# Float16 weights straight from dequantization, and new homes for the cross-attention and FFN tiles, in a one-core decoder layer

## The chip, the cores and the metric

The kernel runs on one core of a Trainium2 chip. The core has five engines that run side by side and meet through semaphores: TensorE (PE, matrix products into PSUM), VectorE (DVE), ScalarE (ACT), GpSimd (POOL) and SyncE (SP, which issues the DMAs). The metric is the device time of one launch in microseconds (us), the median of several runs. Before the change it is 676.97 us (three runs, 676.77 to 679.08).

## What is computed

One decoder layer over x of 8 batches x 128 rows x 512 columns, with a layer norm ahead of each of three parts:

```
x = x + attn(layernorm(x))             # 32 query heads, 8 key/value heads, head size 128, causal softmax
x = x + xattn(ctx, ctx, layernorm(x))  # sim = softmax(ctx @ q.T / 8), softmax over the query index; out = sim @ ctx
x = x + ffn(layernorm(x))              # gate, up: 512 -> 1376; down: 1376 -> 512
ffn:  W[k,n] = q[k,n]*s[g,n] - (z[g,n]+1)*s[g,n],  g = k // 128      # 4-bit q and z, one scale per group of 128
      inter = gate * sigmoid(gate) * up;  out = float16(inter @ Wd)
```

## The kernel before

**Number form.** Every float32 operand of a product is split into two float16 halves, "hi" and "lo" (`split`, `convert`), and a product is three matmuls, hi\*hi, hi\*lo and lo\*hi (`mm3`). The integer weights of the FFN (q - 1 - z) are exact in one float16, so an FFN round has two matmuls: weight x hi, weight x lo.

**Steps.** The attention runs in 64 steps, one for each pair of a key/value group g and a batch b. A step issues on PE the scores (`att_s`), the projections for a later unit of four steps (`proj_parts`), the output projection of the step before (`att_o`) and the product with V (`att_v`). Beside the steps, work is attached to step numbers: weights of the next groups are fetched and converted, the 35 chunks of quantized weights are unpacked in steps 8 to 42 (`dequant`: a shift-and-mask and one scalar_tensor_tensor on VectorE, result in the int8 tiles `n8`), and from step 43 (`XC`) on the context of the cross-attention is loaded (`c_load`), measured (`sumsq`), scaled on GpSimd and split (`c_prep`).

**The tail.** The last group's steps 52 to 55 and 60 to 63 finish one batch each. One step after a batch is done comes `xA` (transposes of the context and of the normed row block by DMA), another step later `xB` (scores and softmax of the cross-attention), then `xC` (its product with the context), with `h3_load`, the layer norm that feeds the FFN.

**The FFN.** From step 60 (`FFN0`) on, FFN rounds are put between attention pieces from a list of events sorted by slot, four slots to a step. `gate_up` makes 22 chains for each half of four batches (11 column tiles x gate, up), each of four rounds, one per quantization group. Between two rounds the PSUM accumulator is multiplied by a ratio of scales, on ScalarE and VectorE in turn, so a chain's next round waits for that. Chain c starts at slot c, its rounds one slot apart. A finished gate chain ends in Silu on ScalarE; an up chain in a product on VectorE, a float16 copy (hi) on VectorE and a subtraction (lo) mostly on GpSimd, into the tile `it`. `down` then makes four chains of eleven rounds.

**Weight copies.** Before its use in the FFN, `nf_load` turns each gate tile from int8 to float16 on ScalarE and each up tile on VectorE (11 + 11), from steps 47 to 55, tiles 3 to 10 into buffers of the attention's query weights (`wqp`); `down_w` does so with 11 down tiles on ScalarE, from steps 52 to 62.

**What sets the order.** The program lists instructions in the order of the code; a planner then orders each engine's queue by readiness and that order. An order written out by hand holds in the tail: PE from step 53 up to step 60, GpSimd from step 53 to the last attention step. Each engine works its queue in order, and SP issues all DMAs of the kernel.

**Pools.** Tiles live in pools that are released and replaced: `deqp` (dequantization) gives way to `xa` (all cross-attention tiles) at step 43, `rawp` (raw weights) to `fw` (float16 FFN weights) and `fp` at step 52 (`FFN_MEM`), and `xa` gives way to `late` (output tiles) near the end. A tile in a replaced pool waits for the last readers of the tiles that it lies upon.

Of the kernel before, what the change touches and what calls it, by code (L numbers as in the profile page):

```python
# [8 lines left out]
F32 = mybir.dt.float32  # L9
F32R = mybir.dt.float32r  # L10
F16 = mybir.dt.float16
BF16 = mybir.dt.bfloat16
I32 = mybir.dt.int32
I8 = mybir.dt.int8
AF = mybir.ActivationFunctionType
ALU = mybir.AluOpType
PSUM = bass.MemoryType.PSUM

P = 128
HQ = 64  # L20
B = 8
H = 512
# [26 lines left out]
XPSCALE = 2.0**15  # L49
ROOT = 2.0**-104  # L50

NF0 = 3


@with_exitstack
def tile_decoder(
# [473 lines left out]
    def run(gen):  # L530
        for _ in gen:
            pass
# [72 lines left out]
    def att_o(g, b):  # L605
# [11 lines left out]


    sF = {}
    n8 = {  # L620
        "g": nqp.tile([P, KT, INTER], I8, name="n8g"),
        "u": nqp.tile([P, KT, INTER], I8, name="n8u"),
        "d": nqp.tile([P, NFT, H], I8, name="n8d"),
    }
    quant = {
        "g": (gq, gz, gs, KT, INTER),
# [111 lines left out]
    def dequant(m, g, c0, c1, after):  # L738
        qsrc = quant[m][0]
        n = c1 - c0  # L740
        rows = min(16, qsrc.shape[0] - g * 16)
        p = rows * 8
        qr = deqp.tile([P, H], I32, name="qr", tag="qr", bufs=2)
        nc.sync.dma_start(
            qr[:p, :n],
            qsrc[g * 16 : g * 16 + rows, c0:c1]
            .rearrange("r n -> r () n")
            .to_broadcast([rows, 8, n]),
        )
        zi = deqp.tile([P, H], I32, name="zi", tag="zi", bufs=2)  # L750
        row = zrow[m] + g
        nc.sync.dma_start(
            zi[:p, :n],
            zt["d"][row : row + 1, c0:c1].to_broadcast([p, n]),
        )
        qi = deqp.tile([P, H], I32, name="qi", tag="qi", bufs=1)
        ins = nc.vector.tensor_scalar(
            qi[:p, :n], qr[:p, :n], sh[:p], 15, ALU.logical_shift_right, ALU.bitwise_and
        )
        issue_after(ins, after)  # L760
        nc.vector.scalar_tensor_tensor(
            n8[m][:p, g, c0:c1], qi[:p, :n], -1.0, zi[:p, :n], ALU.add, ALU.subtract
        )

    chunks = []
# [143 lines left out]
            issue_after(ins, pace["dma"])  # L909

    def c_load(b):
        raw_t["c", b] = c = xa.tile([P, H], F32, name="c", tag="c", bufs=3)
        nc.sync.dma_start(c, cx[b])

    def c_prep(b):
        scales("c", b)
        ctx_scale(b)
        c = raw_t.pop(("c", b))
        ins = nc.gpsimd.tensor_tensor(
            c, c, scx[:, b : b + 1].to_broadcast([P, H]), ALU.mult  # L920
        )
        issue_after(ins, pace["mul"])
        cp = xa.tile([P, 2, H], F16, name="cp", tag="cp", bufs=B)
        split(cp[:, 0, :], cp[:, 1, :], c, nc.gpsimd)
        fl["c", b] = cp

    def norm_T(b, dst):
# [75 lines left out]
    for b in range(B):  # L1003
        at_x(XC + b, lambda b=b: c_load(b))
        at_x(XC + b + 1, lambda b=b: sumsq("c", b, 0, 0))
        at_x(XC + b + 3, lambda b=b: c_prep(b))
        done = steps.index((NG - 1, b))
        tail_x.setdefault((done + 1, 0), []).append(lambda b=b: xA(b))
        tail_x.setdefault((done + 2, 1), []).append(lambda b=b: xB(b))
        tail_x.setdefault((done + 3, 0), []).append(lambda b=b: (xC(b), h3_load(b)))  # L1010

    nf = {}

    def nf_load(m, t):
        w = min(P, INTER - t * P)
        if t < NF0:
            nf[m, t] = fw.tile([P, KT, P], F16, name="nf", tag="nf", bufs=2 * NF0)
        else:
            nf[m, t] = wqp.tile(
                [P, KT, P], F16, name="nf", tag={"g": "wqh", "u": "wql"}[m]  # L1020
            )
        src = n8[m][:, :, t * P : t * P + w]
        if m == "g":
            nc.scalar.copy(nf[m, t][:, :, :w], src)
        else:
            nc.vector.tensor_copy(nf[m, t][:, :, :w], src)

    h3 = {}

# [100 lines left out]
    def gate_up(half, t, m):  # L1130
        w = min(P, INTER - t * P)

        def parts(g):
            return nf[m, t][:, g, :w], h3[half][:, 0, g, :], h3[half][:, 1, g, :]

        def finish(ps):
            sc = sF[m][:w, t, :]
            if m == "g":
                sg = fp.tile([P, TH], F32, name="sg", tag="sg")
                nc.scalar.activation(sg[:w], ps, AF.Silu, scale=sc)  # L1140
                sg_t[half, t] = sg
                return
            sg = sg_t.pop((half, t))
            pr = fp.tile([P, TH], F32, name="pr", tag="pr")
            nc.vector.scalar_tensor_tensor(pr[:w], ps, sc, sg[:w], ALU.mult, ALU.mult)
            if t < NFT - 1:
                it = qp.tile([P, 2, TH], F16, name="it", tag="q" + "hl"[t % 2])
            else:
                it = fw.tile([P, 2, TH], F16, name="it", tag="it", bufs=1)
            eng = nc.vector if half and t >= NFT - 2 else nc.gpsimd  # L1150
            nc.vector.tensor_copy(it[:w, 0, :], pr[:w])  # L1151
            eng.tensor_tensor(it[:w, 1, :], pr[:w], it[:w, 0, :], ALU.subtract)  # L1152
            it_t[half, t] = it

        return Chain(KT, w, lambda: rT[m][:, t, :], parts, finish)

    nd_t = {}

    def down_w(g):
        w = min(P, INTER - g * P)  # L1160
        nd_t[g] = fw.tile([P, H], F16, name="nfd", tag="nfd", bufs=NFT)
        nc.scalar.copy(nd_t[g][:w], n8["d"][:w, g, :])

    def down(half, ct):
        cs = slice(ct * P, (ct + 1) * P)

        def parts(g):
            w = min(P, INTER - g * P)
            it = it_t[half, g]
            return nd_t[g][:w, cs], it[:w, 0, :], it[:w, 1, :]  # L1170

        def finish(ps):
            o = late[0].tile([P, TH], F32, name="oT", tag="oT", bufs=4)
            sc = sF["d"][:, ct, :]
            if ct % 2:
                nc.scalar.activation(o, ps, AF.Copy, scale=sc)
            else:
                nc.vector.tensor_scalar(o, ps, sc, None, ALU.mult)
            pt = bank("a", [P, HB, P], "ps_f")
            for bb in range(HB):  # L1180
                nc.tensor.transpose(pt[:, bb, :], o[:, bb * P : (bb + 1) * P], ident)
            o16 = late[0].tile([P, HB, P], F16, name="o16", tag="o16", bufs=2)
# [12 lines left out]

    late = []

    def free_xa():
        xa.release()
        late.append(pool("late", side="right", reuse_waits="tile"))  # L1200


# [5 lines left out]
    for half, (gs_, ds_) in enumerate([(0, D0), (G1, D1)]):  # L1208
        for c in range(NC):
            ch = gate_up(half, c // 2, "gu"[c % 2])  # L1210
            st = gs_ + (c if half else c + min(c, EARLY))
            for r in range(KT):
                events.append((st + r, 1, c, lambda ch=ch, r=r: ch.emit(r)))
        for ct in range(KT):
            ch = down(half, ct)
            for r in range(NFT):
                st = ct * (0.5 if half else 1)
                events.append((ds_ + st + r, 1, NC + ct, lambda ch=ch, r=r: ch.emit(r)))
    for i, k in [i for i in tail_x if i[0] >= len(steps)]:
        slot = PER_STEP * (i - FFN0) + 1 + 2 * k  # L1220
        events.append((slot, 0, 1, lambda fs=tail_x.pop((i, k)): [f() for f in fs]))
    events.append((PER_STEP * (len(steps) + 5 - FFN0), 0, 1, free_xa))
    events.sort(key=lambda e: e[:3])

    def traced_after(n, engine, earlier):
# [16 lines left out]
    def tail_step(i):  # L1242
# [14 lines left out]
        for f in tail_x.pop((i, 0), ()):  # L1257
            f()
        run(parts)
        slots(3)  # L1260
        att_v(g, b)
        slots(4)
# [15 lines left out]
    for i in range(len(steps)):  # L1278
        known = len(nc.cur_bb.bb.instructions)
        if i == XC:  # L1280
            deqp.release()
            xa = pool("xa", 2, side="right", reuse_waits="tile")
        if i == FFN_MEM:
            rawp.release()
            fw = pool("fw", reuse_waits="tile")
            fp = pool("fp", 2, reuse_waits="tile")
        if i == FFN0:
            xt.update(s="a", o="a")
        pace["dma"] = pt_dma[steps[i + 1]] if i >= TAIL and steps[i + 1 :] and steps[i + 1] in pt_dma else None
# [17 lines left out]
            inter_scale()  # L1307
        for f in x_steps.pop(i, ()):
            f()
        for t in range(NFT):  # L1310
            if i == (FFN_MEM + 1 + t if t < NF0 else XATT - 4 + t):
                nf_load("g", t)
                nf_load("u", t)
        for g in range(NFT):
            if i == FFN_MEM + g:
                down_w(g)
        if i < 5 * HB:
            traced_after(known, last_h.ins.engine, last_h)
        if i == TAIL - 1:
# [8 lines left out]
    for e in events:  # L1328
        e[3]()

    for pl in (late[0], wvp, wkp, wqp, hp, fp, fw, qp, kp, vp, work, wop, psum, dram, nqp):
        pl.release()
    for pl in (small, xres, const):
        pl.release()
# [50 lines left out]
```

## Time and profile before

| | value |
|---|---|
| median of three runs | 676.97 us |
| the profiled execution, its own time | 678.71 us |
| its span, first to last instruction | 676.7 us |
| PE busy | 639.2 us, 94% |
| DVE busy | 480.2 us, 71% |
| ACT busy | 453.2 us, 67% |
| POOL busy | 400.6 us, 59% |
| DMA queue q1 | 42.7% of 16 engines' time |
| mean granted PE clock | 0.989 |

The profile of one execution gives, for each engine, when each instruction started and how long it took; a line number (L...) is that of the kernel's source, and where a helper such as `split` issues the instruction, it is the helper's line. PE instructions overlap, so a PE that is "busy" can still be short of its full rate; how close it is shows in how far apart the starts of neighbouring matmuls lie. Two neighbouring 512-column matmuls start 0.216 us apart where nothing holds them up.

### The profile page before, as it was taken

Reading aid. Unit: us, or ns where it says so; the run is one execution under the profiler, and the core shown is the slowest. Engines: PE = TensorE matmul, PEld = TensorE weight load, DVE = VectorE, ACT = ScalarE, POOL = GpSimd, SP = SyncE. Lnnn points to the kernel's source line nnn. Section 1 sums busy time; section 2 is a strip of 40 time slices with the busy share of each in tenths; the row PEclk is TensorE's granted clock in tenths of the full one; section 3 lists DMA queues with packets and bytes.
Section 4 is the critical chain, followed back from the end, with each engine's and each line's share of the span. In section 5 each row is a group of like instructions: output and inputs, shape, how many; then the busy total and the mean of one; then the engine's idle time right before and its main releaser. Section 6 shows DMA issues by size and latency. Waiting matters only on the chain.

```text
span 676.7 us, 12449 instructions
## 1 busy us (share of the span) xinstructions
PE 639.2 (94%) x3978; PEld 341.6 (50%) x3978; DVE 480.2 (71%) x1504; ACT 453.2 (67%) x1261; POOL 400.6 (59%) x583
## 2 busy tenths in 40 slices
PE   8798999999999999999999999989989988999995
PEld 4365555455555555555555564544545443444442
DVE  6756587765757777676768464676777767988996
ACT  4587486655657574666667666796666667978674
POOL 5658287844747795555588497876775426521310
PEclk9988999999999999999999999999999999999998
DMA  9266344665453756455554525224433232202002
GB/s 309 49 154 176 97 62 117 163 126 148 112 155 87 188 128 157 104 159 127 160 142 109 134 37 136 54 57 87 84 74 56 55 59 48 47 16 62 1 1 62
DMA packets 117757, 69.34 MB, mean 102 GB/s; under 512 B 84174, under 2 KB 100577, under 8 KB 117692
## 3 DMA queue, kind: packets, MB, share of 16 engines
q1 hardware_dynamic: 117692, 68.55, 42.7%
q8 instruction: 31, 0.51, 0.3%
q14 instruction: 34, 0.28, 0.1%
HBM read 42.12 MB, written 2.20 MB: 65 GB/s over the span
## 4 chain that ended last, share of the span: by engine, by line
PE 54%; POOL 14%; DVE 9%; ACT 9%; issue 7%; DMA 6%; SPq 0%; POOLq 0%; DVEq 0%; ACTq 0%
PE ps_o L165 5%; PE ps_c L1114 5%; PE ps_o L163 5%; PE ps_o L164 5%; PE ps_c L1115 5%; PE ps_q L163 5%; PE ps_q L164 5%; PE ps_q L165 4%; DMA pt<-pb 3%; POOL pb L120 3%; POOL s L574 2%; DVE ps_c L1125 2%; POOL wol L120 2%; POOL rawo L357 1%; POOL wql L120 1%
## 5 line engine op out<-in xcount | busy, mean ns | idle before, releaser
L517 ACT ACTIVATE s<-s,negm 128x64 f32<-128x64 f32 (+1 forms) x256 | 93.2, 366 | 35.3 <-DVE negm L560 35.1
L165 PE MATMUL ps_o<-woh,al 128*128 128x512 f16 x256 | 97.3, 380 | 3.4 <-DVE al L120 3.2
L163 PE MATMUL ps_o<-woh,ah 128*128 128x512 f16 x256 | 97.3, 380 | 2.1 <-ACT ah L117 1.9
L163 PE MATMUL ps_q<-hT,wqh 128*128 128x512 f16 x256 | 97.4, 380 | 1.9 <-DVE ql L120 1.0
L165 PE MATMUL ps_q<-hT,wql 128*128 128x512 f16 x256 | 97.3, 380 | 0.0
L164 PE MATMUL ps_o<-wol,ah 128*128 128x512 f16 x256 | 97.3, 380 | 0.0
L164 PE MATMUL ps_q<-hT,wqh 128*128 128x512 f16 x256 | 97.3, 380 | 0.0
L614 DVE SCALAR_TENSOR_TENSOR xr<-ps_o,unsc,xr 128x512 f32<-128x512 f32 x64 | 47.8, 747 | 45.9 <-PE ps_o L165 42.4
L120 POOL TENSOR_TENSOR pb<-s,pb 128x256 f16<-128x256 f32 (+1 forms) x128 | 73.0, 585 | 10.3 <-ACT pb L117 8.6
L560 DVE CUSTOM_DVE_ANT_0 s<-ps_sc,mask,soft 128x64 f32<-128x64 f32 (+1 forms) x256 | 67.2, 310 | 7.3 <-PE ps_sc L165 6.6
L1114 PE MATMUL ps_c<-h,nf 128*128 128x512 f16 (+1 forms) x176 | 66.6, 379 | 3.9 <-ACT sg L1140 1.6
L1115 PE MATMUL ps_c<-h,nf 128*128 128x512 f16 (+1 forms) x176 | 66.6, 379 | 0.0
L574 POOL TENSOR_TENSOR s<-s,rec 128x128 f32<-128x128 f32 (+1 forms) x128 | 62.7, 510 | 4.5
L117 ACT CAST pb<-s 128x128 f16<-128x128 f32 (+1 forms) x128 | 43.2, 350 | 32.3 <-POOL s L574 31.1
L527 POOL TENSOR_SCALAR rec<-rec 128x4 f32<-128x4 f32 x64 | 14.7, 230 | 82.7 <-DVE rec L525 80.5
L120 DVE TENSOR_TENSOR ql<-ps_q,qh 128x512 f16<-128x512 f32 x64 | 43.9, 686 | 25.5 <-ACT qh L117 25.1
L1152 POOL TENSOR_TENSOR it<-pr,it 128x512 f16<-128x512 f32 (+1 forms) x20 | 23.1, 1154 | 63.9 <-DVE it L1151 53.3
L357 POOL TENSOR_TENSOR rawo<-rawo,sco 128x512 f32<-128x512 f32 x30 | 31.1, 1038 | 29.3 <-DVE sco L313 29.3
L120 DVE TENSOR_TENSOR al<-ps_at,ah 128x512 f16<-128x512 f32 x64 | 43.8, 684 | 6.5 <-ACT ah L117 6.3
L517 ACT ACTIVATION_READ_ACCUMULATOR s<-s,negm 128x1 f32 x256 | 48.1, 188 | 0.0
L117 ACT CAST ah<-ps_at 128x512 f16<-128x512 f32 x64 | 37.2, 581 | 14.8 <-PE ps_n L291 7.1
L1123 ACT ACTIVATE ps_c<-ps_c,rTu 128x512 f32<-128x512 f32 (+1 forms) x57 | 36.7, 661 | 12.9 <-PE ps_c L1115 12.3
(219 smaller groups left out, 1733.8 us busy)
## 6 DMA issues: line engine op xcount, KB each, us to landing
rawq<-in_L_attn_w_q_dram SPq DMA_DIRECT2D x8, 1024.0 KB, 6.5
rawo<-in_L_attn_w_o_dram SPq DMA_DIRECT2D x8, 1024.0 KB, 5.4
zi<-zd SPq DMA_DIRECT2D x26, 256.0 KB, 3.7
vd<-v SPq DMA_DIRECT2D x64, 64.0 KB, 2.4
qr<-_L_ffn_down_qweight_dram SPq DMA_DIRECT2D x10, 256.0 KB, 3.3
xr<-in_x_dram SPq DMA_DIRECT2D x8, 256.0 KB, 5.2
rawk<-in_L_attn_w_k_dram SPq DMA_DIRECT2D x8, 256.0 KB, 3.3
rawv<-in_L_attn_w_v_dram SPq DMA_DIRECT2D x4, 512.0 KB, 7.7
```

Source lines behind the costliest of these rows:

```text
L117: a = nc.scalar.copy(hi, src)
L120: b = (lo_eng or nc.vector).tensor_tensor(lo, src, hi, ALU.subtract)
L163: nc.tensor.matmul(ps, lh, rh, start=start and i == 0, stop=False)
L164: nc.tensor.matmul(ps, lh, rl, start=False, stop=False)
L165: nc.tensor.matmul(ps, ll, rh, start=False, stop=stop and i == n - 1)
L357: a = nc.gpsimd.tensor_tensor(raw, raw, wide.to_broadcast(list(raw.shape)), ALU.mult)
L517: exp = nc.scalar.activation(v, v, AF.Exp, bias=negm[:, j : j + 1], scale=-1.0, accum_out=sums[:, j : j + 1],)
L560: nc.vector.tensor_tensor_reduce(view, flat(ps, cols[j]), masks[j // 2], soft_t[g][:, j % 2 : j % 2 + 1], BIG, ALU.add, ALU.min, negm,)
L574: mul = nc.gpsimd.tensor_tensor(v, v, rec[:, 2 * k : 2 * k + 2].unsqueeze(2).to_broadcast([P, 2, (k + 1) * HQ]), ALU.mult,)
L614: return nc.vector.scalar_tensor_tensor(xr[b], ps, unsc_t[g], xr[b], ALU.mult, ALU.add)
L1114: nc.tensor.matmul(ps, lh, rh, start=r == 0, stop=False, skip_group_check=r > 0)
L1115: nc.tensor.matmul(ps, lh, rl, start=False, stop=True, skip_group_check=r > 0)
```

## The change

Six edits, in the order of the code:

- The dequantized weights are kept as float16 for the whole kernel (`nf`, three tiles) instead of int8 (`n8`), and the 33 later copies (`nf_load`, `down_w`) are gone.
- The context lives in a pool of its own, `xc`, opened at step 43 where `xa` was; the other cross-attention tiles (`xa`) move to the pool space opened at step 52, in place of `fw`.
- `c_prep` calls `convert(..., True)`: hi is a scaled copy on ScalarE, lo a scalar_tensor_tensor on VectorE, both straight from the raw context. GpSimd's multiplication and subtraction go.
- `xC` and `h3_load` of the first three batches are issued after the step's projections instead of before.
- The rounds of a gate or up chain lie 1.25 slots apart instead of 1, but for the first seven chains of the first half.
- `it`: of the 22 tiles of the two halves, number 8 to 17 take the query buffers of `qp`, the others the freed query-weight buffers of `wqp`. In the second half the first nine hi copies move from VectorE to GpSimd.

```diff
-    n8 = {
-        "g": nqp.tile([P, KT, INTER], I8, name="n8g"),
+    nf = {
+        "g": nqp.tile([P, KT, INTER], F16, name="nfg"),
...
         nc.vector.scalar_tensor_tensor(
-            n8[m][:p, g, c0:c1], qi[:p, :n], -1.0, zi[:p, :n], ALU.add, ALU.subtract
+            nf[m][:p, g, c0:c1], qi[:p, :n], -1.0, zi[:p, :n], ALU.add, ALU.subtract
         )
...
-        raw_t["c", b] = c = xa.tile([P, H], F32, name="c", tag="c", bufs=3)
+        raw_t["c", b] = c = xc.tile([P, H], F32, name="c", tag="c", bufs=3)
...
-        ins = nc.gpsimd.tensor_tensor(
-            c, c, scx[:, b : b + 1].to_broadcast([P, H]), ALU.mult
-        )
-        issue_after(ins, pace["mul"])
-        cp = xa.tile([P, 2, H], F16, name="cp", tag="cp", bufs=B)
-        split(cp[:, 0, :], cp[:, 1, :], c, nc.gpsimd)
+        cp = xc.tile([P, 2, H], F16, name="cp", tag="cp", bufs=B)
+        hi, lo = convert(cp[:, 0, :], cp[:, 1, :], c, scx[:, b : b + 1], True)
+        issue_after(hi, pace["exp"])
...
-        tail_x.setdefault((done + 3, 0), []).append(lambda b=b: (xC(b), h3_load(b)))
+        tail_x.setdefault((done + 3, 2 if b < HB - 1 else 0), []).append(lambda b=b: (xC(b), h3_load(b)))
...
-    def nf_load(m, t):
...
-            if t < NFT - 1:
-                it = qp.tile([P, 2, TH], F16, name="it", tag="q" + "hl"[t % 2])
+            u = half * NFT + t
+            if 8 <= u < 8 + 10:
+                it = qp.tile([P, 2, TH], F16, name="it", tag="q" + "hl"[u % 2])
+                it = it[:, 0, :], it[:, 1, :]
             else:
-                it = fw.tile([P, 2, TH], F16, name="it", tag="it", bufs=1)
-            eng = nc.vector if half and t >= NFT - 2 else nc.gpsimd
-            nc.vector.tensor_copy(it[:w, 0, :], pr[:w])
-            eng.tensor_tensor(it[:w, 1, :], pr[:w], it[:w, 0, :], ALU.subtract)
+                it = [
+                    wqp.tile([P, TH], F16, name="it" + p, tag="wq" + p) for p in "hl"
+                ]
+            hi_eng = nc.gpsimd if half and t < NFT - 2 else nc.vector
+            lo_eng = nc.vector if half and t >= NFT - 2 else nc.gpsimd
+            hi_eng.tensor_copy(it[0][:w], pr[:w])
+            lo_eng.tensor_tensor(it[1][:w], pr[:w], it[0][:w], ALU.subtract)
...
-    def down_w(g):
...
-                events.append((st + r, 1, c, lambda ch=ch, r=r: ch.emit(r)))
+                events.append((st + (r if c < EARLY and not half else r * 1.25), 1, c, lambda ch=ch, r=r: ch.emit(r)))
...
+        for f in tail_x.pop((i, 2), ()):
+            f()
         slots(3)
...
         if i == XC:
             deqp.release()
-            xa = pool("xa", 2, side="right", reuse_waits="tile")
+            xc = pool("xc", 2, side="right", reuse_waits="tile")
         if i == FFN_MEM:
             rawp.release()
-            fw = pool("fw", reuse_waits="tile")
             fp = pool("fp", 2, reuse_waits="tile")
+            xa = pool("xa", 2, reuse_waits="tile")
...
-                nf_load("g", t)
-                nf_load("u", t)
...
-                down_w(g)
```

More of the change, by code (lines that the diff above doesn't have):

```diff
@@ L13 @@
 I32 = mybir.dt.int32
-I8 = mybir.dt.int8
 AF = mybir.ActivationFunctionType
@@ L50 @@
 ROOT = 2.0**-104
-NF0 = 3
 @with_exitstack
@@ L619, in tile_decoder @@
     sF = {}
-    n8 = {
-        "g": nqp.tile([P, KT, INTER], I8, name="n8g"),
-        "u": nqp.tile([P, KT, INTER], I8, name="n8u"),
-        "d": nqp.tile([P, NFT, H], I8, name="n8d"),
+    nf = {
+        "g": nqp.tile([P, KT, INTER], F16, name="nfg"),
+        "u": nqp.tile([P, KT, INTER], F16, name="nfu"),
+        "d": nqp.tile([P, NFT, H], F16, name="nfd"),
     }
@@ L1009, in tile_decoder @@
         tail_x.setdefault((done + 2, 1), []).append(lambda b=b: xB(b))
-        tail_x.setdefault((done + 3, 0), []).append(lambda b=b: (xC(b), h3_load(b)))
-    nf = {}
-    def nf_load(m, t):
[L1015 to L1026, printed above, removed]
+        tail_x.setdefault((done + 3, 2 if b < HB - 1 else 0), []).append(lambda b=b: (xC(b), h3_load(b)))
     h3 = {}
@@ L1133, in parts @@
         def parts(g):
-            return nf[m, t][:, g, :w], h3[half][:, 0, g, :], h3[half][:, 1, g, :]
+            return nf[m][:, g, t * P : t * P + w], h3[half][:, 0, g, :], h3[half][:, 1, g, :]
         def finish(ps):
@@ L1145, in finish @@
             nc.vector.scalar_tensor_tensor(pr[:w], ps, sc, sg[:w], ALU.mult, ALU.mult)
-            if t < NFT - 1:
-                it = qp.tile([P, 2, TH], F16, name="it", tag="q" + "hl"[t % 2])
-            else:
-                it = fw.tile([P, 2, TH], F16, name="it", tag="it", bufs=1)
-            eng = nc.vector if half and t >= NFT - 2 else nc.gpsimd
-            nc.vector.tensor_copy(it[:w, 0, :], pr[:w])
-            eng.tensor_tensor(it[:w, 1, :], pr[:w], it[:w, 0, :], ALU.subtract)
+            u = half * NFT + t
+            if 8 <= u < 8 + 10:
+                it = qp.tile([P, 2, TH], F16, name="it", tag="q" + "hl"[u % 2])
+                it = it[:, 0, :], it[:, 1, :]
+            else:
+                it = [
[5 more added lines that the diff above has]
+            lo_eng.tensor_tensor(it[1][:w], pr[:w], it[0][:w], ALU.subtract)
             it_t[half, t] = it
         return Chain(KT, w, lambda: rT[m][:, t, :], parts, finish)
-    nd_t = {}
-    def down_w(g):
-        w = min(P, INTER - g * P)
-        nd_t[g] = fw.tile([P, H], F16, name="nfd", tag="nfd", bufs=NFT)
-        nc.scalar.copy(nd_t[g][:w], n8["d"][:w, g, :])
     def down(half, ct):
@@ L1169, in parts @@
             it = it_t[half, g]
-            return nd_t[g][:w, cs], it[:w, 0, :], it[:w, 1, :]
+            return nf["d"][:w, g, cs], it[0][:w], it[1][:w]
         def finish(ps):
@@ L1196, in tile_decoder, with free_xc @@
     late = []
-    def free_xa():
-        xa.release()
+    def free_xc():
+        xc.release()
         late.append(pool("late", side="right", reuse_waits="tile"))
@@ L1219, in tile_decoder @@
     for i, k in [i for i in tail_x if i[0] >= len(steps)]:
-        slot = PER_STEP * (i - FFN0) + 1 + 2 * k
+        slot = PER_STEP * (i - FFN0) + (1, 3, 2)[k]
         events.append((slot, 0, 1, lambda fs=tail_x.pop((i, k)): [f() for f in fs]))
-    events.append((PER_STEP * (len(steps) + 5 - FFN0), 0, 1, free_xa))
+    events.append((min(PER_STEP * (len(steps) + 5 - FFN0), D0 + NFT - 1), 0, 1, free_xc))
     events.sort(key=lambda e: e[:3])
@@ L1309, in tile_decoder @@
             f()
-        for t in range(NFT):
-            if i == (FFN_MEM + 1 + t if t < NF0 else XATT - 4 + t):
-                nf_load("g", t)
-                nf_load("u", t)
-        for g in range(NFT):
-            if i == FFN_MEM + g:
-                down_w(g)
         if i < 5 * HB:
@@ L1329, in tile_decoder @@
         e[3]()
-    for pl in (late[0], wvp, wkp, wqp, hp, fp, fw, qp, kp, vp, work, wop, psum, dram, nqp):
+    for pl in (late[0], wvp, wkp, wqp, hp, xa, fp, qp, kp, vp, work, wop, psum, dram, nqp):
         pl.release()
```

## The prediction

> **What bounds the kernel now.** I read the strip of 40 slices first (a slice is 16.9 us; a digit is tenths of it):
>
> ```profile
> PE   8798999999999999999999999989989988999995
> DVE  6756587765757777676768464676777767988996
> ACT  4587486655657574666667666796666667978674
> POOL 5658287844747795555588497876775426521310
> PEclk9988999999999999999999999999999999999998
> ```
>
> PE is the fullest engine nearly everywhere, so a change pays only where PE stands still. "Busy" hides part of that, so I took the starts of all matmuls from the PE timeline and compared neighbours: 512 columns start 0.216 us apart when nothing is late, fewer columns in proportion. What lies beyond that is lost: 59 us in all. 17.5 us of it is in the first 60 us (loading, untouched), 12.7 in 60 to 440, 5.1 in 440 to 460, 8.3 in 460 to 520, 0.5 in 520 to 540, 11.1 in 540 to 600, 1.4 in 600 to 660 and 2.4 after it, before the last stores. The change acts from about 405 on. So 25 us, 440 to 600, are what it can win from. The windows there (PE, PEld, DVE, ACT, POOL busy; then PE clock):
>
> ```profile
> 440.00:460.00 20.00, 17.18 (x105) 9.39 (x104) 14.29 (x51) 19.71 (x58) 14.27 (x21) 0.91 0.27 66
> 460.00:520.00 60.00, 54.93 (x388) 29.76 (x387) 42.71 (x166) 36.09 (x115) 40.84 (x64) 1.00 0.40 75
> 540.00:600.00 60.00, 53.76 (x269) 24.05 (x268) 49.37 (x107) 47.90 (x78) 29.75 (x33) 1.00 0.28 48
> 600.00:660.00 60.00, 59.69 (x284) 28.19 (x283) 54.77 (x97) 44.15 (x71) 10.39 (x9) 1.00 0.08 21
> ```
>
> In the first ScalarE is full and the clock is low; in the third DVE and ACT are 80% busy; in the last PE loses nothing, though DVE is 91% busy.
>
> **Part A, the copies of the weights.** The removed groups, and the one that `c_prep` gets instead:
>
> ```profile
> L1026 DVE CAST nf<-n8u 128x512 f16<-128x512 int8 x10 | 8.7, 888 | 3.1 <-PE ps_q L165 3.1
> L1024 ACT CAST nf<-n8g 128x512 f16<-128x512 int8 x10 | 6.1, 615 | 3.1 <-PE ps_q L164 3.1
> L1162 ACT CAST nfd<-n8d 128x512 f16<-128x512 int8 x10 | 5.6, 612 | 0.0
> L352 DVE SCALAR_TENSOR_TENSOR wql<-rawq,scq,wqh 128x512 f16<-128x512 f32 x4 | 3.4, 841 | 2.0 <-ACT wqh L351 2.0
> ```
>
> With the odd last tiles, 22 casts leave ACT (some 13 us) and 11 leave DVE (some 9 us). What matters is where they stand. ACT's timeline, then PE's:
>
> ```profile
> 449.76 2.16 ACT L1162 CAST nfd<-n8d 128x512 f16<-128x512 int8 x4
> 451.82 0.61 ACT L1024 CAST nf<-n8g 128x512 f16<-128x512 int8 x1
> 452.34 0.57 ACT L117 CAST qh<-ps_q 128x512 f16<-128x512 f32 x1
> ```
> ```profile
> 451.22 0.28 PE L597 MATMUL ps_at<-pt,vd 128*128 128x256 f16 x1 [1.05 <-DMA pt<-pb]
> ...
> 453.70 0.28 PE L163 MATMUL ps_v<-wvh,hT 128*128 128x256 f16 x1 [1.76 <-DVE softx L323]
> ...
> 456.55 0.63 PE L164 MATMUL ps_o<-wol,ah 128*128 128x512 f16 x1
> ```
>
> From 445.87 to 452.34 ACT does little but such casts, the hi copy of the query projection stands behind them, and its bank is free for ps_v only at 453.7. Between 449.95 and 457.65 PE spent 7.70 us on work of 2.76 us (1 ps_sc, 5 ps_at and 12 ps_v of 0.108, 4 ps_o of 0.216): 4.9 us lost, 3.1 standing and 1.8 at half rate (ps_v 0.21 apart, ps_o 0.42). Here a rule bears on the sum. The Trainium skill ("TensorE: Matmul & The Clock Gate", Part 1) has the clock halve after at least one idle window of about 3.4 us. By the row it fell after idles of 1.05 and 1.76 us with five matmuls between. By the rule the 1.8 us would have another cause and stay (gain 2.4); by the row it goes with the stall. I take the row, and leave 0.7 us for a smaller stall of the same copies: **4.2 us**, ends 0 and 4.9.
>
> In 460 to 520 six gate casts go to ACT straight ahead of a query copy. The cast at 475.21 needs only the last matmul but one of the projection, its twin on DVE at 475.42 the last: it starts 0.21 us before the query copy could and holds ACT 0.52 us start to start, so it delays that by 0.3, six times: 1.8 us. PE there loses 6.0 us in stalls of over 0.4 us on ql, qh or al (0.55, 0.86, 0.51, 0.58, 1.26, 1.17, 0.41, 0.65), so each has something to give. The DVE casts hide behind the query copy (DVE done 476.2, ACT 476.3) and give nothing there. What is late next is al itself, for which att_o's third matmul waits.
>
> The dequantization's own instruction keeps its inputs and its 0.78 to 0.95 us for 512 or fewer elements; whether a float16 result costs more than int8 no row shows: 35 of them, -0.1 to +0.1 us each, hidden by PE either way: 0.
>
> **Part B, xC behind the projections** (steps 55 to 57). Nothing is added; three matmuls (0.65 us) move between the projection and att_v, so ACT has done the query copy when ps_at is ready and ah starts at once. These steps hold al stalls of 0.58, 1.26 and 1.17. The query copy and ah have about 0.25 us of overlap to lose in each: **0.7 us**. The residual update and h3's norm come 2.6 us later (12 matmuls); h3 is first used at 518.7 and these three's transposes were issued at 487.0, 497.8 and 507.5; the fourth, at 515.6, isn't moved. Ends of A's 1.8 and B together: 0 and 5.
>
> **Part C, the context on ACT and DVE.** POOL loses 8 x (1.05 + 1.16) = 17.7 us between 413 and 473; ACT's 8 copies become scaled ones, 0.62 to 0.72 (L351's row): +0.8 us; DVE gains 8 x 0.84 = 6.7 us, less than the 9 us it loses by A. The cover is PE's lead: DVE is about 65% busy there. The result feeds xo and cT, wanted from 476 on. A smaller effect: with `xa` opened at step 52, the context transposes that SP issued early, at 417 and 437, come in the tail, two issues of 1.2 us more on SP, which there has about four of these in a 10 us step. At 417 that issue stood ahead of a pt transpose, and PE lost 1.6 us at 421.5 behind it. Ends -2 and +1.6; I take **+0.5**. The new `xa` lies on raw weights whose last reader, wol on POOL, ends at 445.8, twenty us before the first norm writes: no wait.
>
> **Part D, chains 1.25 slots apart.** With four chains in flight, rounds come in the order oldest first; a chain's next round starts 3 places of 0.43 us after the last, which leaves 0.86 us for the scaling. At 1.25 the order turns to newest first and the distance is 5 places: 1.73 us. A scaling takes 0.66 (ACT) or 0.75 (DVE) and two hand-overs, so at 1.73 a queue may be one instruction late without PE noticing. In 540 to 580 PE loses 6 us on such waits (sg 0.74 and 1.00, pr, ps_c) and 2.7 on qT's transposes. But the change removes no instruction there: DVE and ACT keep 49.4 and 47.9 busy us of 60, eight table loads of 1.28 among them, and PE that arrives earlier waits longer for qT; also 1.5 rounds (0.65 us) less stand ahead of each xs. Six PSUM banks turn over in 24 places, a chain now needs 16 and its ending. Ends -0.7 and +4.5; I take **1.3**. The first seven chains stay, and in 600 to 660 there is nothing to win.
>
> **Part E, `it`.** Nine hi copies (0.42 each) leave DVE for POOL. The Trainium skill ("GPSIMD Engine Reference", 3.1) speaks against it: elementwise work on GpSimd is about twice as slow. The nearest row, the one-input h<-xr of POOL, is 0.77, so 0.35 us later a tile by row, 0.4 by rule; bare, nine would cost 3.2 or 3.8. The cover: POOL is 17% busy there, and a tile waits for its down round while the other chains run; POOL needs 0.77 + 1.15 for a tile, PE 3.46 for its 16 matmuls. 0, as is the 3.8 us less on DVE, where PE loses nothing. The other buffers remove no wait that shows: 0.
>
> **Sum.** 4.2 + 1.8 + 0.7 + 0.5 + 1.3 = 8.5 us off the span of 676.7: 668.2. The profiled run's own time was 678.71, 2.0 above its span, and 1.7 above the median; taken off the median of 676.97 the sum gives **668.5 us**.
>
> **Rivals.**
> - **Only part of the burst** (0.16). Copies of pb, cp and ah crowd ACT anyway; 3 us come back, al stalls stay: 674.0. For it: at 451.22 PE waited for a DMA, not for ACT. Against: ACT had 15 of the removed casts in the 10.6 us from 445.9. The planner's other order on DVE could do the same.
> - **More** (0.12). D works as its distance says and A, B to their ends: 4.9 + 4 + 4 + 1.5 = 14.4, 662.6. Against: DVE's 82%.
> - **Slower** (0.12). Place: DVE between 405 and 475. The new scalar_tensor_tensor reads two SBUF inputs; beside a busy POOL its row for wvl shows 1.13 us. If it stands ahead of ql or al each time, with 0.1 more on ACT, 8 x 1.23 = 9.8 us come onto the path; less A's 4.2: 682.6. It eats the burst's gain from 4 of the 8 places on. Against: PE lost little in 390 to 440 with DVE two thirds free.
> - The forecast's own case, 664.5 to 672.5, has 0.60.
>
> A measurement tells about 0.5% from no change: 673.6 to 680.4. Faster: 0.60 + 0.12 + 0.05 of the first rival; same: the rest of it, 0.11; slower 0.12. The range 663 to 674.5 leaves out the slow case and half of the fast one.
>
> **What would show it.** A: no PE gap over 1 us between 440 and 460, clock 1.00 there, and no casts L1024, L1026, L1162. B: al waits of under 3 us in 460 to 520 in sum. C: POOL some 17 us less busy. D: PE's sg and ps_c waits in 540 to 580 down by a third, qT's not. E: PE still without gaps over the last gate/up stretch. I am wrong if the 450 stall comes back under another name, or if c's lo stands where ql stood.

## The result and the profile after

The kernel after takes 671.0 us (median of 4 runs, 669.6 to 672.25) against 677.73 us for the kernel before on the same chip (4 runs). The ratio is 0.9899, with a 95% interval of 0.9867 to 0.9931: 6.8 us less, with 4.7 and 9.0 us as the ends of the interval. The forecast was 668.5 us.

| | before | after |
|---|---|---|
| profiled execution, its own time | 678.71 us | 669.99 us |
| its span | 676.7 us | 668.2 us |
| mean granted PE clock | 0.989 | 0.999 |
| PE time lost between matmul starts, about | 59 us | 51 us |
| DVE, ACT, POOL busy | 480.2, 453.2, 400.6 us | 478.1, 443.3, 389.4 us |

The strip of 40 slices of the kernel after (a slice is now 16.7 us):

```profile
PE   7798999999999999999999999999998989899996
DVE  6756687765757776675778465677676779889896
ACT  4587486655757575656678566875566478977774
POOL 5668297744747795556588587753577247422520
PEclk9999999999999999999999999999999999999999
```

The hole that PE had in slice 27 (an 8 at 440 to 457 us) is gone, and so is ACT's 9 beside it. The windows (PE, PEld, DVE, ACT, POOL busy, PE clock, DMA share, GB/s) say the same in numbers:

```profile
440.00:460.00 20.00, 19.71 (x132) 11.24 (x131) 15.59 (x61) 12.14 (x37) 7.38 (x16) 1.00 0.39 85
460.00:520.00 60.00, 55.99 (x400) 30.30 (x399) 42.33 (x168) 37.70 (x129) 36.71 (x63) 1.00 0.44 76
540.00:600.00 60.00, 55.27 (x277) 25.44 (x276) 52.77 (x110) 49.32 (x82) 28.99 (x31) 1.00 0.27 46
600.00:660.00 60.00, 58.74 (x280) 27.76 (x279) 53.66 (x93) 42.77 (x69) 15.79 (x18) 1.00 0.07 18
```

In the first window PE works 27 matmuls more than before and ACT falls from 19.7 to 12.1 us. Counted from matmul starts as in the prediction, PE loses 0.8 us there (before 5.1), 7.6 in 460 to 520 (8.3), 2.6 in 520 to 540 (0.5), 7.1 in 540 to 600 (11.1) and 2.6 in 600 to 660 (1.4). The windows are fixed in time and after is some us ahead in them, so its last one holds more of the final rounds.

The spans differ by 8.5 us, the very sum of the prediction, but that is partly luck. At the first output projection, before any dequantized weight is written, the run after is already 2.4 us ahead, and at step 42, up to which the change touches only the type of those weights, 2.1 us: in the loading stage PE ran at a clock of 0.74 in 35 to 40 us and 0.69 in 55 to 60 us in the profiled run of before, and at 1.00 in that of after. So the change itself is worth 6.4 us of the span, which agrees with the medians. To keep such luck out, the next table takes each run's place at step 42 as zero. It gives the start of a step's first output-projection matmul against before (us, negative is earlier), for one execution of each of the runs that are described below:

| run | step 52 | step 57 | step 62 | end of the span |
|---|---|---|---|---|
| after | -3.5 | -5.4 | -4.5 | -6.4 |
| after, copies put back (`copies`) | -1.1 | -2.0 | -1.3 | -2.9 |
| after without B (`no_b`) | -3.5 | -1.3 | -0.8 | -2.8 |
| after without C (`no_c`) | -1.9 | -2.5 | -1.0 | -0.3 |
| `no_c` with 5 context buffers (`no_c_c5`) | -4.8 | -5.6 | -4.4 | -4.2 |
| after without D (`no_d`) | -3.2 | -5.1 | -4.3 | -4.5 |
| after without E (`no_e`) | -3.7 | -5.6 | -4.9 | -4.8 |
| A alone (`a_pools`) | -2.8 | +0.3 | +0.9 | -1.4 |
| A with 5 context buffers (`a_pools_c5`) | -4.5 | -1.7 | -0.8 | -3.0 |
| D alone (`d_only`) | -0.3 | -0.2 | -0.2 | -0.7 |

### The profile page after: what moved, and what is told of

Read it like the earlier page. It is cut to its first block, busy times and chain, and to the rows that moved or that the text cites. A ratio compares the mean times of both kernels' runs of the same rounds, so it can differ in the third digit from the quotient of the medians.

```text
span 668.2 us, 12402 instructions
## 1 busy us (share of the span) xinstructions
PE 632.3 (95%) x3978; PEld 339.1 (51%) x3978; DVE 478.1 (72%) x1492; ACT 443.3 (66%) x1239; POOL 389.4 (58%) x576
## 4 chain that ended last, share of the span: by engine, by line
PE 49%; POOL 18%; issue 9%; DMA 8%; DVE 8%; ACT 7%; SPq 0%; POOLq 0%; DVEq 0%; ACTq 0%
PE ps_c L1093 6%; PE ps_c L1094 6%; PE ps_o L163 5%; PE ps_o L161 5%; PE ps_o L162 5%; DMA pt<-pb 4%; PE ps_q L161 4%; PE ps_q L163 4%; PE ps_q L162 4%; POOL pb L118 4%; POOL s L572 3%; DMA rawq<-in_L_attn_w_q_dram 2%; POOL wql L118 2%; POOL wol L118 2%; POOL rawo L355 2%
## 5 line engine op out<-in xcount | busy, mean ns | idle before, releaser
L118 POOL TENSOR_TENSOR pb<-s,pb 128x256 f16<-128x256 f32 (+1 forms) x128 | 71.9, 577 | 11.1 <-ACT pb L115 8.4
L115 ACT CAST qh<-ps_q 128x512 f16<-128x512 f32 x64 | 36.8, 575 | 15.3 <-PE ps_q L163 15.2
L1104 DVE TENSOR_SCALAR ps_c<-ps_c,rTg 128x512 f32<-128x512 f32 (+1 forms) x56 | 40.5, 750 | 7.2 <-PE ps_c L1094 7.1
L161 PE MATMUL ps_sc<-k,qh 128*128 128x128 f16 (+1 forms) x256 | 41.2, 206 | 2.7 <-ACT qh L115 2.6
```

The lines of the kernel that those rows point to most:

```text
L115: a = nc.scalar.copy(hi, src)
L118: b = (lo_eng or nc.vector).tensor_tensor(lo, src, hi, ALU.subtract)
L161: nc.tensor.matmul(ps, lh, rh, start=start and i == 0, stop=False)
L1104: nc.vector.tensor_scalar(ps, ps, sc, None, ALU.mult)
```

## The experiments

The letters A to E are the parts of the prediction. Times are medians, ratios are against the kernel before on the same chip with their 95% intervals, and "worth" is a difference of two ratios times 678 us. A part's worth "in company" is what its removal from the kernel after costs (for A, the return of the copies); "alone" is what it gives when it is added to the kernel before. The ratio of after itself is known to 0.3%, so a worth in company is good to 2 or 3 us, and the same error of after stands in all five of them.

### A alone, and the copies at another time

`a_pools` is the kernel after with B, C, D and E undone: float16 weights, the moved pools and the new homes of `it` stay, so it measures these together.

```diff
-        hi, lo = convert(cp[:, 0, :], cp[:, 1, :], c, scx[:, b : b + 1], True)
-        issue_after(hi, pace["exp"])
+        convert(cp[:, 0, :], cp[:, 1, :], c, scx[:, b : b + 1])
...
-        tail_x.setdefault((done + 3, 2 if b < HB - 1 else 0), []).append(...)
+        tail_x.setdefault((done + 3, 0), []).append(...)
...
-                events.append((st + (r if c < EARLY and not half else r * 1.25), 1, c, ...))
+                events.append((st + r, 1, c, ...))
...
-            hi_eng = nc.gpsimd if half and t < NFT - 2 else nc.vector
+            hi_eng = nc.vector
```

> The changed kernel with edits B, C, D and E undone: float16 weights, the pools and the homes of it stay. Theory 1 (the weight copies are what PE stood for): 4 to 6 us under the kernel before, no PE gap over 1 us between 440 and 460, PE clock 1.00 there. Theory 2 (the gain comes from the moves of xC, the context and the chains): under 2 us, and the waits of 0.5 to 1.3 us on al in 460 to 520 are still there. Without chains 1.25 slots apart, 540 to 600 loses about 11 us of PE rate as before.

678.14 us, ratio 0.9997 (0.9984 to 1.001): A alone gains nothing (good to 0.9 us), where the forecast had 6.0 us for it. The view of PE's waits in 460 to 520 (us in total, times, longest) shows half of the reason. Kernel before:

```profile
PE ps_o L165 <- DVE al L120: 3.2, 4, 1.1
PE ps_sc L165 <- DVE ql L120: 0.8, 2, 0.5
PE ps_v L163 <- DVE ql L120: 0.4, 1, 0.4
...
PE ps_xo L163 <- ACT xph L970: 0.2, 1, 0.2
```

A alone:

```profile
PE ps_xo L163 <- DVE xpl L965: 2.0, 3, 1.3
PE ps_xo L161 <- ACT xph L964: 1.3, 3, 0.6
PE ps_o L163 <- DVE al L118: 0.8, 2, 0.6
PE ps_sc L163 <- DVE ql L118: 0.5, 1, 0.5
```

The waits for al and ql fall from 4.4 to 1.3 us; the prediction had named them, with 1.8 us, for the six casts ahead of the query copies. But the waits of xC's first product for the two halves of the cross-attention's softmax, xph and xpl, rise from 0.2 to 3.3 us. PE arrives earlier and meets another late operand. The other half of the reason is in 440 to 460, where PE still loses about 3.3 us. The waits of ACT and of SP's queue in 436 to 460 of A alone:

```profile
ACT junk L259 <- DMA c<-in_ctx_dram: 6.8, 3, 2.7
SPq L911 <- POOL cp L118: 10.0, 3, 7.2
```

For the first, the same view of after has 1.1 us, and that of before 1.7 us. The timeline of A alone over all engines shows where the longest comes from and what it does to PE (start, duration, engine, instruction, and in brackets the idle time before it):

```profile
450.21 1.16 POOL L118 TENSOR_TENSOR cp<-c,cp 128x512 f16<-128x512 f32 x1 [0.86 <-ACT cp L115]
...
451.39 0.33 SPq L911 DMA_DIRECT2D c<-in_ctx_dram  x1
...
454.14 0.63 ACT L259 ACTIVATE junk<-c 128x512 bf16<-128x512 f32 x1 [2.74 <-DMA c<-in_ctx_dram]
...
455.54 0.58 ACT L115 CAST ah<-ps_at 128x512 f16<-128x512 f32 x1
...
456.18 0.39 PE L161 MATMUL ps_o<-woh,ah 128*128 128x512 f16 x1 [1.41 <-ACT ah L115]
```

The subtraction on POOL ends at 451.37, and 0.02 us later SP issues the next context load, because it was the last reader of one of three context buffers. The load is there at 454.1. Until then ACT's square of that context stands at the head of ACT's queue, with ah behind it, and PE stands 1.41 us for ah. That is the reading that I call R from here on: **the buffers of the context, not the copies alone, keep ACT from PE's work**.

`paced` is the kernel before with its 33 copies kept, but each bound to the exponential (ACT) or the residual update (VectorE) of its own step, so that they can't pile up.

```diff
-            nc.scalar.copy(nf[m, t][:, :, :w], src)
+            issue_after(nc.scalar.copy(nf[m, t][:, :, :w], src), pace["exp"])
...
-            nc.vector.tensor_copy(nf[m, t][:, :, :w], src)
+            issue_after(nc.vector.tensor_copy(nf[m, t][:, :, :w], src), pace["row"])
...
-        nc.scalar.copy(nd_t[g][:w], n8["d"][:w, g, :])
+        issue_after(nc.scalar.copy(nd_t[g][:w], n8["d"][:w, g, :]), pace["exp"])
```

> The kernel before, with its 33 weight copies kept but each tied behind its own step's last exponential (ACT) or residual update (DVE), so that the planner cannot bring the down copies forward into one heap at 446 to 456. Theory 1a (the heap, not the work, cost the 4.9 us): 3 to 5 us under the kernel before, clock 1.00 between 440 and 460. Theory 1b (the 22 us of copies as such cost it): no gain, or up to 3 us slower, since the down copies then fall into steps 52 to 62 where ACT and DVE are fuller.

684.4 us, ratio 1.0075 (1.0052 to 1.0099). Spreading the copies makes it worse. In the profiled execution (680.84 us, one of the two fastest) PE loses about 3.6 us in 440 to 460, where it lost 5.1 with the pile, but in 440 to 520 it waits 1.6 us for ah, once, and 7.0 us for xph and xpl. So undoing the pile was not worth the forecast's 4.2 us. It doesn't clear the pile of blame, for two other things changed with it: the copies now stand in the steps where xph is made, and ACT waits 5.7 us for the context's load in 436 to 460, where it waited 1.7 before.

### C and D taken out of the kernel after

`no_c` puts the context back on GpSimd (the first part of the diff of `a_pools`).

> The changed kernel with the context again multiplied and split on GpSimd. If the direct form is worth its 0.5 us: 0 to 1 us slower than the changed kernel, GpSimd 17 us busier. Rival (VectorE's new instruction stands ahead of ql or al, and is why 386 to 440 lost 0.7 us against the kernel before): 0.5 to 2 us faster than the changed kernel, PE's lost time in 380 to 440 back from 4.8 to 4.0 us.

677.4 us, ratio 0.998 (0.9968 to 0.9993). C is worth 5.5 us in company, where the forecast had 0.5; neither line of the expectation had a loss of this size. ACT's wait for the context load is back, 6.9 us in 436 to 460.

`no_d` puts the rounds back to one slot apart (the third part of that diff).

> The changed kernel with all chains 1 slot apart again. Theory D (more distance between the rounds of a chain lets the scaling be late): 2 to 4 us slower than the changed kernel, PE loses 10 to 11 us in the 60 us from the first gate round of the ring on, against 7.1. Rival (the 540 to 600 gain comes from elsewhere, DVE and ACT hold the rate): within 1 us of the changed kernel. The changed kernel's new losses in 520 to 540 and 600 to 660 (2.0 and 1.3 us more than before) go away if D is their cause, and stay otherwise.

673.28 us, ratio 0.9935 (0.9911 to 0.9958): D is worth 2.4 us, forecast 1.3. Most of it arises after step 62, as the table of places shows (the gap between `no_d` and after grows from 0.2 to 1.9 us). PE's waits in 540 to 580, in before:

```profile
PE ps_xs L163 <- DMA qT<-hb: 2.2, 3, 1.3
PE ps_c L1114 <- ACT sg L1140: 1.6, 3, 0.8
...
PE ps_c L1114 <- ACT ps_c L1123: 0.3, 1, 0.3
PE ps_c L1114 <- DVE ps_c L1125: 0.2, 1, 0.2
```

without D:

```profile
PE ps_xo L161 <- ACT xph L965: 1.6, 1, 1.6
PE ps_c L1093 <- DVE ps_c L1104: 1.3, 2, 1.1
PE ps_xs L161 <- DMA qT<-hb: 1.1, 2, 0.8
PE ps_c L1093 <- DVE pr L1124: 0.7, 2, 0.5
PE ps_c L1093 <- ACT ps_c L1102: 0.4, 1, 0.4
```

and in after:

```profile
PE ps_c L1093 <- ACT sg L1119: 2.3, 2, 1.8
PE ps_c L1093 <- ACT ps_c L1102: 0.7, 1, 0.7
PE ps_c L1093 <- DVE pr L1124: 0.5, 2, 0.3
PE ps_c L1093 <- DVE ps_c L1104: 0.2, 1, 0.2
```

Against `no_d` the waits for a scaled accumulator fall from 1.7 to 0.9 us, which is what a longer distance between rounds should do; but before had only 0.5. Those for xph and qT are gone from this stretch, and one Silu (sg) is 1.8 us late instead. It stands behind two loads of activation tables on ACT, one for the softmax's exponential and one back for Silu:

```profile
565.89 1.28 ACT L515 ACT_TABLE_LOAD   x1
...
567.70 1.28 ACT L1119 ACT_TABLE_LOAD   x1
568.99 0.69 ACT L1119 ACTIVATE sg<-ps_c,sFg 128x512 f32<-128x512 f32 x1
```

So the runs show that D pays in company, by about its forecast, but not that it pays by the longer distance.

### Is it the buffer?

`no_c_c5` leaves the context on GpSimd but gives it five buffers; `a_pools_c5` does so with A alone. `plus_c5` adds the two buffers to the kernel after itself.

```diff
-        raw_t["c", b] = c = xc.tile([P, H], F32, name="c", tag="c", bufs=3)
+        raw_t["c", b] = c = xc.tile([P, H], F32, name="c", tag="c", bufs=5)
```

> The run no_c (context split on GpSimd) with five instead of three buffers for the raw context. Theory R (what no_c loses at 447 to 458 is a chain of waits: GpSimd's late last subtraction holds the buffer, SP cannot issue the next load, and the Square of the next context block stands at the head of ScalarE's queue with ah and qh behind it): the loads come early, ScalarE's wait of 6.8 us on the context's load falls under 2, PE's lost time in 440 to 460 from 3.3 to under 1.5, and the time falls 2 to 5 us under no_c, to 672 to 675. Rival (GpSimd's 17 us of work as such): within 1 us of no_c's 677.4.

> The weights in float16 and the moved pools alone, context on GpSimd, no move of the normalisation, one-slot rounds, copies on VectorE, but with 5 context buffers in place of 3. Theory R (the buffer wait ate what the missing copies gave): most of the 4.7 us that two more buffers gave without the new context split come back here too: 673 to 675, with no wait of ScalarE's Square for the context DMA over 1 us at 436 to 460. Rival (removing the copies is worth nothing, the buffers only helped the other parts of the change): 677 to 678.5.

> The kernel after with 5 context buffers in place of 3. Theory R: the context wait left in the kernel after is 1.1 us at 436 to 460 and PE loses 0.8 us there, so the buffers can give 0.8 at most: 670.3 to 671.5. Rival (more prefetch, more gain, as without the new context split): 667 to 669.

`no_c_c5`: 673.32 us, ratio 0.9928 (0.9902 to 0.9954), 3.5 us better than `no_c`. `a_pools_c5`: 673.38 us, ratio 0.9946 (0.9931 to 0.9961), 3.5 us better than `a_pools`. `plus_c5`: 671.54 us, ratio 0.9918 (0.9901 to 0.9934), no better than after. So R holds: two buffers give 3.5 us (good to 2 and to 1.3 us) wherever POOL lets go of the context late, and nothing where C has already removed that. ACT's waits in 436 to 460 of `a_pools_c5` show the sides changed:

```profile
ACT pb L115 <- POOL s L572: 4.1, 5, 2.2
ACT qh L115 <- PE ps_q L163: 3.7, 1, 3.7
ACT junk L259 <- DMA c<-in_ctx_dram: 0.8, 2, 0.6
```

ACT now waits 3.7 us for PE; with three buffers it was PE that waited for ACT. PE's only listed wait there is 0.5 us. In the table, A with five buffers is 4.5 us ahead at step 52, one more than after. It then gives 2.8 us back by step 57, the steps of B.

### B, E, and more of the same

`no_b` issues xC ahead of the projections everywhere (second part of the diff of `a_pools`). `no_e` takes the hi copies back to VectorE (fourth part). `plus` has five context buffers and the fourth batch's xC behind the projections too, `2 if b < HB else 0`.

> The changed kernel with xC ahead of the projections in all steps. Theory B: PE stands before xC on the softmax's halves (xph, xpl), as it did for 3.8 us in the run without B to E; 1.5 to 3.5 us slower than the changed kernel. By the prediction's term 0.7 us. Rival: within 0.5 us.

> The changed kernel with the nine hi copies of the second half back on VectorE. Prediction: no difference, within 0.7 us; VectorE 3.8 us busier, PE's lost time in the last 60 us of gate and up within 0.5 us of the changed kernel's. Rival: the 2.6 us that PE loses in 600 to 660 in the changed kernel (1.35 before) come from E, and the run is 1 us faster.

> The changed kernel, with five buffers for the raw context and xC of the fourth batch behind the projections as well. If theory R and B hold further: the stall of 1.1 us on xph and xpl at 501 goes, and the 1.1 us wait of ScalarE on the context's load; 0.5 to 2 us faster than the changed kernel. Rival: the planner's other order gives it back, within 0.7 us.

`no_b`: 674.29 us, ratio 0.994 (0.9919 to 0.9962), so B is worth 2.8 us, and the table puts the loss between steps 52 and 57, where B acts. PE's waits of `no_b` in 460 to 520:

```profile
PE ps_xo L163 <- DVE xpl L966: 2.7, 4, 1.3
PE ps_xo L161 <- ACT xph L965: 1.0, 3, 0.6
PE ps_o L163 <- DVE al L118: 0.8, 2, 0.6
```

In after the first two are 0.3 and 0.5 us. So B gains by giving xph and xpl the time of the projection's matmuls. It does nothing for al, 0.8 us without it and 1.2 with it.

`no_e`: 671.68 us, ratio 0.9908 (0.9878 to 0.9939), not to be told from after. `plus`: 672.5 us, ratio 0.9914 (0.9889 to 0.9939), nor is this. In it the waits for xph and xpl are gone from 460 to 520, but PE loses 5.2 us in 540 to 560, where after loses 3.1; which of its two edits does that, `plus_c5` doesn't tell, since it is no slower than after.

Both runs also lose time behind PE's last FFN product. In `no_e` that product starts at 659.3 us, 2.1 us earlier than in after, and yet the span is 1.2 us longer. All four output tiles are finished together there, and the third has to wait for the first one's store, because `ob` has two buffers; in after the first two come 4.2 us ahead of the others. In `no_e`, then in after:

```profile
664.30 1.76 DVE L1165 TENSOR_TENSOR ob<-xr,o 128x128 f32<-128x128 f32 x8 [1.65 <-DMA out_dram<-ob]
```
```profile
663.06 1.80 DVE L1165 TENSOR_TENSOR ob<-xr,o 128x128 f32<-128x128 f32 x8 [1.88 <-ACT o L1161]
```

`plus` has the same 1.65 us. These are single executions, and more buffers for `ob` were not tried.

### A inside the kernel after, D without the rest

`copies` is the kernel after, with 33 copies of the weights into scratch tiles that nothing reads, in the old places. They are extra work; the FFN still uses `nf`.

```diff
+    def nf_load(m, t):
+        w = min(P, INTER - t * P)
+        cpy = xa.tile([P, KT, P], F32 if m == "u" else F16, name="nx" + m, tag="nx" + m, bufs=1)
+        src = nf[m][:, :, t * P : t * P + w]
+        if m == "g":
+            nc.scalar.copy(cpy[:, :, :w], src)
+        else:
+            nc.vector.tensor_copy(cpy[:, :, :w], src)
...
+        for t in range(NFT):
+            if i == (FFN_MEM + 1 + t if t < 3 else XATT - 4 + t):
+                nf_load("g", t)
+                nf_load("u", t)
+        for g in range(NFT):
+            if i == FFN_MEM + g:
+                down_w(g)
```

> The kernel after, with the 33 weight copies put back in their old places as work that nothing reads (22 on ScalarE, 11 on VectorE, into scratch tiles); everything else of the change stays. It asks what the copies are worth once the buffer wait is gone. Theory R (the copies only filled holes that the late context load had left in ScalarE's queue; with the holes closed they are in the way): the forecast's 6 us come out here, 675 to 677.5, with PE stalls of 3 us or more at 445 to 460. Rival (the copies are free at any time, the planner finds room for them): within 1 us of the kernel after, 670.5 to 672.

674.07 us, ratio 0.9958 (0.9944 to 0.9973): the copies cost 4.0 us, between the two theories. On ACT a copy takes as long as in before (0.61 us), on VectorE less (0.41 us, where before had a median of 0.65), and the planner places all 22 of ACT's between 441 and 467. So the old places are those in the program; on the chip the six gate casts that stood ahead of query copies between 464 and 513 in before stand earlier. PE's timeline at 455 to 459:

```profile
455.63 0.27 PE L161 MATMUL ps_v<-wvh,hT 128*128 128x256 f16 x1 [0.59 <-DVE ql L118]
458.62 0.39 PE L161 MATMUL ps_o<-woh,ah 128*128 128x512 f16 x1 [1.29 <-ACT ah L115]
```

and PE loses 3.3 us in 440 to 460 instead of 0.8. The stall that the prediction went after comes back with the copies, at somewhat over half its size.

`d_only` is the kernel before with the 1.25 slots alone (from the eighth chain of the first half on, as in the change; the expectation says the fourth).

> The kernel before with the gate and up rounds paced at 1.25 slots from the fourth chain on, nothing else changed. Theory (the pacing pays by itself, as much as taking it out of the kernel after cost: 2.3 us): 675 to 676.5. The forecast's own figure for it, 1.3 us, is 676 to 677.2. Rival (it pays only together with the later normalisation): 677.5 to 679.

678.03 us, ratio 1.0004 (0.9992 to 1.0015): nothing, though D is worth 2.4 us in company. The two differ by no more than the error of the second.

## Why the prediction was right, and where its sum was not

The direction and the likeliest case were right: a gain of about 1%, with PE's losses in 440 to 600 down from 25.0 to 18.1 us and no PE gap over 1 us left in 440 to 460. The time came out 2.5 us longer than forecast, and the sum of 8.5 us lies inside the measured 4.7 to 9.0. That it came so near is in part luck, for the parts did not come out as they were priced:

| part | forecast | worth in company | alone |
|---|---|---|---|
| A, weight copies | 6.0 | 4.0 | 0.2 (3.7 with 5 context buffers) |
| B, xC behind the projections | 0.7 | 2.8 | |
| C, context on ACT and DVE | 0.5 | 5.5 | |
| D, 1.25 slots | 1.3 | 2.4 | -0.3 |
| E, hi copies on POOL | 0 | 0.6, within error | |
| together | 8.5 | 6.8 | |

- **What doesn't hold is the plus sign.** A gives 0.2 us alone and 4.0 in company, with errors of 0.9 and 2.4, so its worth depends on the rest; two context buffers give 3.5 us without C and nothing with it. The five worths in company add up to 15.3 us and all at once give 6.8, but the error of after counts five times in that sum (some 11 us), so the sum alone would prove nothing. Each part takes one of several late operands away, and PE gains only as far as the next. The prediction asked "what is late next" for A and answered "al"; the runs showed the context's square (while C is missing) and xph and xpl (while B is missing). Its own sign of being wrong, the stall at 450 under another name, is there in A alone: 1.41 us for ah, then 0.84 for al.
- **A came out 2 us smaller, which is within the error**, and the 1.8 us in 460 to 520 is not measured by `copies`, whose casts stand earlier. One piece that was over-sized can be seen. Of the stall's 4.9 us, 1.8 were charged to PE's half clock. `d_only` has the same stall (1.05 and 1.78 us) at full clock, and its next matmul then waits 0.96 us for ah: PE was so early that the time bought nothing. It loses 4.8 us in 440 to 460, before 5.1. So the half clock was worth 0.3 us, not 1.8.
- **C was put down to the wrong resource.** The prediction priced instructions on ACT, DVE and POOL, and found PE's lead to cover them. Most of what C gives is the early release of a buffer (3.5 of the 5.5 us come back with two more): the raw context's last reader is now DVE, and no longer POOL with its subtraction. The price of DVE's new instruction was near what the "slower" rival had (1.05 us in the mean, 1.13 there). Twice it stands straight ahead of ql, at 431.6 and 450.3 us, as that rival feared, but no listed wait of PE for DVE follows any of the eight within 2.5 us. The stall at 421.5 us was laid to an issue of cT on SP. In after that issue is gone from there (the first cT is at 438.6) and PE still waits 1.1 us at 420.0 for ah. ACT's square of a weight tile had waited 1.4 us for its 1 MB load ahead of it.
- **B works, by another wait.** Named was al, for 0.7 us; it is xph and xpl, for 2.8.
- **D has about the forecast's size, but not its signs.** The waits for sg and for scaled accumulators, in sum 2.1 us before in 540 to 580, are 3.2 after, where a fall by a third was named, and qT's, said to stay, fall from 2.2 to nothing in that stretch (one of 0.8 us ahead of it is left).
- **E doesn't show in the time, as forecast,** though `no_e` loses at the end, in the wait for a store, part of what PE gained there, so E's price for PE stays open. POOL's hi copies take 0.61 us, less than the 0.77 taken from a neighbour's row.
- **The float16 result costs the dequantization nothing that matters**, as forecast: its 35 instructions take 28.7 us, before 28.0.
- POOL is 11.2 us less busy, where 17 were named: the nine hi copies that come to it (5.5 us) were left out of that figure.

What stays open: with five buffers but without C the FFN still ends later. `no_c_c5` is as far as after at step 57, and 2.2 us behind at the end; PE loses 10.2 us in 540 to 600 there, after 7.1. A wait of 1.7 us for one accumulator scaled on ACT is part of it. Which work stood ahead on ACT was not tried. `plus` and `plus_c5` beat the kernel before, not the kernel after.

## What to carry to other kernels

Price a removed instruction by the wait that comes second, and follow that wait through buffers: who reads the tile last, which load that releases, and which instruction stands at the head of an in-order queue until it lands. When several edits touch the same chain, measure each by taking it out of the whole, because alone it may show nothing while the others still hold PE. A wait that vanishes and one that appears can cancel, as in A alone, so look at the list of waits, not at the time alone.

## What the hardware showed

PE's clock under equal work was not repeated from run to run. Windows of 2 us around the same stall (the granted clock is the column after the busy times), in before:

```profile
452.00:454.00 2.00, 0.30 (x3) 0.28 (x4) 1.01 (x5) 2.00 (x5) 0.96 (x1) 1.00 0.00 0
454.00:456.00 2.00, 2.00 (x11) 1.21 (x9) 0.16 (x1) 2.00 (x6) 0.93 (x1) 0.51 0.00 0
456.00:458.00 2.00, 2.00 (x7) 0.72 (x7) 1.11 (x2) 2.00 (x8) 1.28 (x3) 0.64 0.35 79
```

and in D alone:

```profile
450.00:452.00 2.00, 0.22 (x3) 0.09 (x2) 0.90 (x5) 2.00 (x5) 1.04 (x1) 1.00 0.00 0
452.00:454.00 2.00, 1.40 (x12) 1.01 (x12) 0.31 (x3) 2.00 (x6) 0.71 (x1) 1.00 0.00 0
454.00:456.00 2.00, 1.52 (x7) 0.56 (x8) 1.07 (x3) 2.00 (x8) 1.34 (x3) 1.00 0.26 39
```

The same two idles, 1.05 and then 1.76 or 1.78 us with five matmuls between, brought the clock to half in one execution and not in the other. So neither the prediction's row nor the rule that it was weighed against (the Trainium skill, "TensorE: Matmul & The Clock Gate", Part 1: an idle window of about 3.4 us) says by itself when it falls. In the loading stage, which none of the runs changes, the mean clock of 20 to 40 us was 0.91 in before and 1.00 in after, for the same part of the program, and the four runs of after fall in two pairs: clock 0.999 with 669.6 and 670.0 us, and about 0.99 with 672.0 and 672.3. Between two profiles the spans can differ by 2 us through this luck alone, a third of this change's gain.
